# Decoder layer: the next tile's attention scores between a tile's quantised rows and their product with the context

## The chip, the cores and the metric

The kernel runs on one core of a Trainium2 chip. The metric is the device time of one execution in microseconds (us), as the median of several runs. TensorE is PE in the profile, VectorE is DVE, ScalarE is ACT, GpSimd is POOL, and SP is the engine that issues most of the loads.

## The reference, cut to what matters

The input x has 2 x 512 token rows of 1024 numbers. Three stages follow each other, each with a residual and a layer norm:

```python
# 1. attention inside each token, between its 32 "d" positions, over 8 groups of heads
q = einsum('bse,edh->bsdh', x, Wq) + bq          # k, v likewise, repeated 4 times over the heads
attn = softmax(einsum('bsdh,bseh->bsde', q, k) / sqrt(32))
x = layernorm(x + einsum('bsde,bseh->bsdh', attn, v))
# 2. product with the context, both sides rounded to 8 bits
fake_quant = lambda x, s, z: (clip(round(x / s + z), 0, 255) - z) * s
x = layernorm(x + matmul(fake_quant(x), fake_quant(ctx)))     # ctx: 2 x 1024 x 1024
# 3. feed-forward block with a routed part
h = relu(x @ up_w) ** 2                            # 1024 -> 2048
shared = h @ down_w
routed = ((x @ fc1_w) @ expert_w) * (sum of the two largest of x @ gate_w) @ fc2_w
x = layernorm(x + layernorm(shared + routed) * gamma + beta)
```

## The kernel before

**Tiles and blocks.** The 1024 token rows are cut into 8 tiles of 128 rows (one row for each partition). Two tiles make a block, so there are four blocks. Stages 1 and 2 work tile by tile; stage 3 works block by block, for blocks 0 and 1 with plain products (`ffn`), and for blocks 2 and 3 together with fewer, combined products (`ffn_pair`).

**The token path of one tile.** `scores` (L435, L441) multiplies and sums q and k on VectorE in four chunks. `exponentials` (L450, L451, L454) takes the row maximum, subtracts it on VectorE, and takes Exp on ScalarE. `attend` (L458 to L487) sums the exponentials, multiplies them with v on VectorE in four chunks (L466, L472), and adds the result to the tile xc; `normalise_aside` then normalises xc on ScalarE, with a small power on GpSimd. `cross` quantises the rows on ScalarE into `a` (L598), lets a DMA from ScalarE's queue transpose them into `aT` (L601), and multiplies `aT` with the quantised context `cq` on TensorE (L611, the tile py, in two halves). VectorE adds the row sums' share (r at L604, L605) and the product (L615) to xc, and ScalarE normalises again. `hand_over` transposes xc into x2T, the input of the feed-forward products. Tile 1, the last one before block 0 can start, takes another way through `cross`, called hurried: it quantises on VectorE and transposes on TensorE.

**The feed-forward of a block.** `ffn` runs 16 up products (L768, relu and square on ScalarE at L786 and L787), 4 products with fc1 (VectorE multiplies them by the routing at L797), and 20 steps of down products (L982). `finish` then reads the sums on VectorE (L295 to L939).

**What sets the order.** The program is emitted by generators. `token_path` emits tile by tile; `fill` emits the projections of tiles 2 to 7, beside tiles 0 and 1; `ffn` emits a block's products, beside tiles 2 to 7. Each `yield` hands over a weight, meant as microseconds, and a loop advances the token path while its sum of weights times `PACE` is below the sum of the feed-forward's weights. A scheduler then fixes the order on each engine at build time: it prefers what was emitted earlier, but lets later work pass where it believes that the earlier work is not ready. An edge overrides it: instructions traced under `tc.issue_after(x)` stay behind x on x's engine. `behind_products` uses such an edge to keep py behind the last feed-forward product that had been emitted by then.

**Buffers.** py takes a bank from `spare_bank`: of ps_dn while a block's up products run (`phase` "up"), of ps_mm, which has two banks, while its down products run. The up products and the routing take ps_mm banks as well. xc has 6 buffers, prod, s, qk and v two each, and aT and cq one each. The second half of the rows needs a second quantised context: `context_beside` makes it on ScalarE while block 0 runs, once py of tile 3 has been emitted, and tile 4's `cross` is emitted only when it is complete (`made`).

**Loads.** xc(t) is loaded from SP's queue, q, k and v of tile t from GpSimd's queue (`fetch_qkv`), the weights from SP's queue.

Of the kernel before, what the change touches and what calls it, by code (L numbers as in the profile page):

```python
# [9 lines left out]
F32 = mybir.dt.float32  # L10
BF16 = mybir.dt.bfloat16
AF = mybir.ActivationFunctionType
ALU = mybir.AluOpType
# [3 lines left out]
P = 128  # L17
# [10 lines left out]
def kernel(  # L28
# [24 lines left out]
    nc = tc.nc  # L53

    B, S, E = x.shape
    _, D, H = wq.shape
# [11 lines left out]
    NT = B * S // P  # L68
    TB = 2
# [1 line left out]
    NBLK = NT // TB  # L71
    HALF = 512
    DC = 8
    PACE = 0.64
    GW = 32
    NK = NI + NL

# [3 lines left out]
    xf = x.flatten_outer_dims()  # L81
# [4 lines left out]
    xpool = ctx.enter_context(tc.tile_pool(name="xc", bufs=6))  # L86
# [34 lines left out]
    bv_ge = frontp.tile([P, G, D], F32, name="bv_ge")  # L121
# [45 lines left out]
    def new_qkv(t, away):  # L167
        pool, bufs = (attp, KEPT) if away else (tokp, 2)
        qk = pool.tile([P, 2 * DG], F32, tag="s12" if away else "qk", name=f"qk_{t}", bufs=bufs)
        v = pool.tile([P, G, D], F32, tag="s4" if away else "v", name=f"v_{t}", bufs=bufs)  # L170
        return qk, v

    def fetch_qkv(t):
        qk, v = new_qkv(t, False)
        nc.gpsimd.dma_start(qk, qkv_d[t, :, 0 : 2 * DG])
        nc.gpsimd.dma_start(v.rearrange("p g e -> p (g e)"), qkv_d[t, :, 2 * DG :])
        qkv[t] = qk, v
# [48 lines left out]
    qkv = {}  # L226
    xTs = [load_xT(0)]
    ps0 = [projection_psum(t) for t in range(TB)]
    for k in range(KE):
        stage = work.tile([P, E], F32, tag="work", name=f"wq_{k}")  # L230
        nc.sync.dma_start(wqkv[k][:, DG : 2 * DG], wk2[ts(k, P), :])
        last = nc.sync.dma_start(stage, wq2[ts(k, P), :])
# [33 lines left out]
    ns12 = const.tile([P, 1], F32, name="ns12")  # L266
# [3 lines left out]
    s12d2 = const.tile([P, 1], F32, name="s12d2")  # L270
# [157 lines left out]
    def scores(t, qk, behind=None):  # L428
        q3 = qk[:, 0:DG].rearrange("p (d g) -> p d g", g=G)
        k3 = qk[:, DG : 2 * DG].rearrange("p (e g) -> p e g", g=G)  # L430
        s = tokp.tile([P, D, D], F32, tag="s", name=f"s_{t}", bufs=2)
        for c in range(D // DC):
            prod = tokp.tile([P, DC * D * G], F32, tag="prod", name=f"pqk_{t}_{c}", bufs=2)
            with tc.issue_after(behind.ins) if behind is not None else ExitStack():
                nc.vector.tensor_tensor(  # L435
                    prod.rearrange("p (d e g) -> p d e g", d=DC, g=G),
                    q3[:, ts(c, DC), :].unsqueeze(2).to_broadcast([P, DC, D, G]),
                    k3.unsqueeze(1).to_broadcast([P, DC, D, G]),
                    ALU.mult,
                )  # L440
            nc.vector.tensor_reduce(  # L441
                s[:, ts(c, DC), :].rearrange("p d e -> p (d e)"),
                prod.rearrange("p (c g) -> p c g", g=G), AX.X, ALU.add,
            )
            yield 4.6
        return s

    def exponentials(t, s):
        smax = small.tile([P, D], F32, tag="smax", name=f"smax_{t}")
        nc.vector.tensor_reduce(smax, s, AX.X, ALU.max)  # L450
        nc.vector.tensor_tensor(  # L451
            s, s, smax.unsqueeze(2).to_broadcast([P, D, D]), ALU.subtract
        )
        nc.scalar.activation(s, s, AF.Exp, scale=INV_SQRT_D)  # L454

    def attend(t, xc, s, v):
        den = small.tile([P, D], F32, tag="den", name=f"den_{t}")
# [112 lines left out]

        return tc.issue_after(lately[0].ins) if lately[0] is not None else ExitStack()

    def cross(t, xc, cq, crow):
        hurried = t == TB - 1
        tmp = work.tile([P, E], F32, tag="work", name=f"qt_{t}")
        a = attp.tile([P, E], BF16, tag="a", name=f"a_{t}")
        aT = tokp.tile([P, KC, P], BF16, tag="aT", name=f"aT_{t}")
        if hurried:

            quantise(a, xc, tmp, rs1, z1)  # L580
            yield 2.2
            pt = ps_tr.tile([P, KC, P], BF16, tag="tr", name=f"pta_{t}")
            with behind_products():
                for k in range(KC):
                    nc.tensor.transpose(pt[:, k, :], a[:, ts(k, P)], identb)
            nc.scalar.copy(aT, pt)
            yield 1.0
            total = ps_tr.tile([P, 2], F32, tag="tr", name=f"pr_{t}")
            for k in range(KC):
                nc.tensor.matmul(  # L590
                    total, aT[:, k, :], onesb[:, 0:2], start=(k == 0), stop=(k == KC - 1)
                )
            total = total[:, 0:1]
        else:
            total = small.tile([P, 1], F32, tag="total", name=f"total_{t}")
            for _ in below_top(tmp, xc, tmp, rs1, z1):
                pass
            nc.scalar.activation(  # L598
                a, tmp, AF.Identity, scale=-1.0, bias=code_down, accum_out=total
            )  # L600
            nc.scalar.dma_start_transpose(aT, a)  # L601
            yield 12.0
        r = small.tile([P, 1], F32, tag="r", name=f"r_{t}")
        nc.vector.tensor_mul(r, total, s12d2)  # L604
        nc.vector.scalar_tensor_tensor(xc, xc, r, crow, ALU.add, ALU.add)  # L605
        sums = small.tile([P, 2], F32, tag="sum2", name=f"sum2_{t}")
        for h in range(E // HALF):
            py = spare_bank(f"py_{t}_{h}")
            with behind_products():
                for k in range(KC):  # L610
                    crossed[t] = nc.tensor.matmul(  # L611
                        py, aT[:, k, :], cq[:, k, ts(h, HALF)], start=(k == 0), stop=(k == KC - 1)
                    )
            xh = xc[:, ts(h, HALF)]
            nc.vector.scalar_tensor_tensor(  # L615
                xh, py, ns12, xh, ALU.mult, ALU.add,
                accum_out=None if hurried else sums[:, h : h + 1],
            )
        if hurried:
            last = normalise(xc, f"2_{t}")  # L620
            yield 6.0
        else:
            yield 3.0
            last = yield from normalise_aside(xc, sums, f"2_{t}")
            yield 6.0
        return last

    def token_path():


        batch = ahead = None
        for blk in range(NBLK):
            xcs = []
            x2T = []
            for i in range(TB):
                t = blk * TB + i
                xc = xpool.tile([P, E], F32, tag="xc", name=f"xc_{t}")
                nc.sync.dma_start(xc, xf[ts(t, P), :])
                qk, v = qkv.pop(t)
                if 0 < t < NT - 1:  # L640
                    fetch_qkv(t + 1)
                if t == TB:
                    first = last
                if ahead is None:

                    ahead = scores(t, qk, first if t >= TB else None)
                while True:
                    try:
                        step = next(ahead)
                    except StopIteration as done:  # L650
                        s = done.value
                        break
                    yield step
                exponentials(t, s)
                if t < TB:
                    nc.vector.tensor_add(v, v, bv_ge)
                yield 3.1
                ahead = None
                if t == 0:

                    ahead = scores(1, qkv[1][0])
                    yield next(ahead)
                yield from attend(t, xc, s, v)
                if t % (S // P) == 0:
                    b = t // (S // P)
                    while len(made) < (b + 1) * KC:
                        yield 1.0
                    batch = cqs[b], context_row(b, cqs[b])
                last = yield from cross(t, xc, *batch)

                def hand_over(blk=blk, t=t, i=i, xc=xc, x2T=x2T):
                    if not x2T:
                        pool, tag = (attp, "x2T") if blk <= PAIR else (pools["late"], "x2T_late")
                        x2T.append(pool.tile([P, KE, NB], F32, tag=tag, name=f"x2T_{blk}"))
                    with behind_products():
                        transpose_f32(x2T[0][:, :, ts(i, P)], xc, f"x2_{t}")

                    nc.gpsimd.dma_start(xc, ln_beta.partition_broadcast(P), accum_op=ALU.add)

                if t == 0 or up_to[0] < blk or blk > PAIR:
                    held.append((blk, hand_over))
                else:
                    hand_over()
                xcs.append(xc)
            yield blk, xcs, x2T
# [406 lines left out]

    pools = {}
    tokens = token_path()
    rest = fill()

# [28 lines left out]
    for blk in range(PAIR):  # L1127
        while len(ready) <= blk:
            w_tok += advance()
        for weight in ffn(*ready[blk]):  # L1130
            w_ffn += weight
            while alive and w_tok * PACE < w_ffn:
                step = advance()
# [45 lines left out]
```

## Time and profile before

| what | us |
|---|---|
| three runs | 736.18, 737.22, 740.0; median 737.22 |
| the profiled execution | 733.81, of which the span is 731.8 |
| TensorE busy | 696.0 |
| VectorE busy | 545.1 |
| ScalarE busy | 240.0 |
| start of block 0's first up product | 149.7 |
| start of block 1's first up product | 315.5 |
| start of the pair's first product | 474.9 |

The profile is of one execution. Its span runs from the first to the last instruction; the 2 us beside it are the execution's start and end. A row such as "L611 PE MATMUL py<-cq,aT x16" gives the line of the kernel, the engine, the operation, the tile written and the tiles read, and a bracket after it the idle time of that engine just before it, with what ended it. fp32 products show as two records each, so that one up product of 8 matmuls is 16 records.

### The profile page before, as it was taken

The page shows a single profiled execution, that of the slowest core. Times are in us where ns is not written, and L with a number is a line of the kernel's source. Part 1 is how long each engine was busy: PE and PEld are TensorE (multiplying, and loading weights), DVE is VectorE, ACT ScalarE, POOL GpSimd, SP SyncE. Part 2 cuts the span into 40 slices and gives each one's busy share as a digit, 9 for nine tenths or more (in the row PEclk, how much of TensorE's full clock was granted, in tenths as well). Part 3 has the DMA queues.
Part 4 walks back from the last instruction along what each step waited for, and adds up shares of the span by engine and source line. Part 5 has one row for each costly group of instructions (what it writes and reads, how often), then busy time and mean ns, then how long its engine had stood idle before and what let it go on. Part 6 is the DMA issues. An engine that isn't in the chain of part 4 may idle for free. (4 is left out here: it accounts for less than half of the span.)

```text
span 731.8 us, 7278 instructions
## 1 busy us (share of the span) xinstructions
PE 696.0 (95%) x2803; PEld 493.8 (67%) x2812; DVE 545.1 (74%) x619; ACT 240.0 (33%) x389; POOL 64.0 (9%) x96
## 2 busy tenths in 40 slices
PE   6999999999799899999899999999999999999992
PEld 3666654478686344478686444588888888888882
DVE  4799986899989779999899950455454663779736
ACT  2097733222553394428525240311522100000001
POOL 2001211200101020002001000100000000001001
PEclk9999999999999999999999999999999999999996
DMA  8999533785535485456357345441333134555501
GB/s 284 346 297 379 125 45 106 246 285 161 162 116 156 140 256 211 143 167 228 92 168 186 120 169 177 132 109 58 123 107 116 57 116 173 173 173 202 201 1 57
DMA packets 71554, 120.05 MB, mean 164 GB/s; under 512 B 10640, under 2 KB 44944, under 8 KB 71520
## 3 DMA queue, kind: packets, MB, share of 16 engines
q1 hardware_dynamic: 57344, 98.84, 40.0%
q0 software_dynamic: 6496, 18.39, 9.7%
q10 hardware_dynamic: 7680, 2.36, 1.5%
q8 instruction: 22, 0.36, 0.2%
q14 instruction: 12, 0.10, 0.0%
HBM read 106.73 MB, written 11.01 MB: 161 GB/s over the span
## 5 line engine op out<-in xcount | busy, mean ns | idle before, releaser
L982 PE MATMUL pd<-dn,h 128*128 128x512 f32 x320 | 138.8, 592 | 0.0
L768 PE MATMUL pu<-x2T,up 128*128 128x256 f32 x512 | 112.7, 380 | 1.1 <-DMA up<-in_L_ffn_up_w_dram 1.1
L982 PEld LDWEIGHTS pd<-dn,h 128*128 128x128 f32 x320 | 60.5, 190 | 72.9 <-issue 72.2
L768 PEld LDWEIGHTS pu<-x2T,up 128*128 128x128 f32 x512 | 96.6, 190 | 15.7 <-ACT relu L786 1.8
L435 DVE TENSOR_TENSOR pqk<-qk 128x2048 f32<-128x2048 f32 x32 | 72.3, 2283 | 0.0
L441 DVE TENSOR_REDUCE s<-pqk 128x256 f32<-128x2048 f32 x32 | 72.3, 2277 | 0.0
L466 DVE TENSOR_TENSOR pav<-s,v 128x2048 f32<-128x2048 f32 x32 | 72.3, 2280 | 0.0
L472 DVE TENSOR_REDUCE o<-pav 128x64 f32<-128x2048 f32 x32 | 71.9, 2265 | 0.0
L152 PE MATMUL pqk<-wqkv,xT 128*128 128x512 f32 x128 | 65.2, 610 | 1.1 <-DVE wqkv L233 0.8
L1022 DVE TENSOR_TENSOR tt<-dn 128x1024 f32<-128x1024 f32 x20 | 24.3, 1220 | 24.5 <-DMA dn<-in_L_ffn_down_w_dram 15.7
L157 PEld LDWEIGHTS pv<-wqkv,xT 128*128 128x128 f32 x128 | 24.3, 190 | 24.2 <-issue 22.0
L1068 PE MATMUL ps<-dn,h 128*128 128x256 f32 x160 | 40.4, 379 | 0.0
L1068 PE MATMUL ps<-tt,h 128*128 128x256 f32 x160 | 40.4, 379 | 0.0
L1068 PE MATMUL ps<-dn,s 128*128 128x256 f32 x160 | 40.4, 379 | 0.0
L611 PE MATMUL py<-cq,aT 128*128 128x512 bf16 x121 | 29.9, 395 | 10.2 <-DMA aT<-a 9.8
L1080 ACT COPY y<-ps 128x256 f32<-128x256 f32 x4 | 1.5, 373 | 109.9 <-PE ps L1068 109.9
L157 PE MATMUL pv<-wqkv,xT 128*128 128x256 f32 x128 | 35.6, 379 | 0.0
L615 DVE SCALAR_TENSOR_TENSOR xc<-py,ns,xc 128x512 f32<-128x512 f32 x16 | 11.9, 748 | 28.7 <-PE py L611 28.4
L1068 PEld LDWEIGHTS ps<-dn,h 128*128 128x128 f32 x160 | 30.4, 190 | 4.1
L1068 PEld LDWEIGHTS ps<-dn,s 128*128 128x128 f32 x160 | 30.4, 190 | 4.1
L1068 PEld LDWEIGHTS ps<-tt,h 128*128 128x128 f32 x160 | 30.4, 190 | 4.1
L326 POOL TENSOR_TENSOR rstd<-ve,neg_half 128x1 f32<-128x1 f32 x18 | 14.3, 795 | 213.4 <-ACT ve L324 212.6
(204 smaller groups left out, 1022.1 us busy)
## 6 DMA issues: line engine op xcount, KB each, us to landing
dn<-in_L_ffn_down_w_dram SPq DMA_DIRECT2D x32, 1024.0 KB, 5.1
up<-in_L_ffn_up_w_dram SPq DMA_DIRECT2D x16, 1024.0 KB, 5.3
dn<-e SPq DMA_DIRECT2D x8, 1024.0 KB, 5.0
pair<-in_L_ffn_up_w_dram SPq DMA_DIRECT2D x8, 1024.0 KB, 5.3
fc<-in_L_ffn_fc_w_dram SPq DMA_DIRECT2D x6, 1024.0 KB, 5.9
xs<-in_x_dram SPq DMA_DIRECT2D x8, 512.0 KB, 7.2
wq<-in_L_attn_Wq_dram SPq DMA_DIRECT2D x8, 512.0 KB, 5.8
xc<-in_x_dram SPq DMA_DIRECT2D x8, 512.0 KB, 9.6
```

The source lines that it names most:

```text
L152: projecting[0] = nc.tensor.matmul(pqk, xT[:, k, :], wqkv[k][:, 0 : 2 * DG], start=(k == 0), stop=(k == KE - 1))
L157: nc.tensor.matmul(pv[:, :DG], xT[:, k, :], wqkv[k][:, 2 * DG : 3 * DG], start=(k == 0), stop=(k == KE - 1),)
L326: nc.gpsimd.tensor_tensor(rstd, ve, neg_half, ALU.pow)
L435: nc.vector.tensor_tensor(prod.rearrange("p (d e g) -> p d e g", d=DC, g=G), q3[:, ts(c, DC), :].unsqueeze(2).to_broadcast([P, DC, D, G]), ...
L441: nc.vector.tensor_reduce(s[:, ts(c, DC), :].rearrange("p d e -> p (d e)"), prod.rearrange("p (c g) -> p c g", g=G), AX.X, ALU.add,)
L466: nc.vector.tensor_tensor(prod.rearrange("p (d g e) -> p d g e", d=DC, g=G), s[:, ts(c, DC), :].unsqueeze(2).to_broadcast([P, DC, G, D]), ...
L472: nc.vector.tensor_reduce(o[:, ts(c, DC), :].rearrange("p d g -> p (d g)"), prod.rearrange("p (c e) -> p c e", e=D), AX.X, ALU.add,)
L611: crossed[t] = nc.tensor.matmul(py, aT[:, k, :], cq[:, k, ts(h, HALF)], start=(k == 0), stop=(k == KC - 1))
L768: lately[0] = nc.tensor.matmul(ps[:, :NB], ws[:, k, wcols], xT[:, k, :], start=(k == 0), stop=(k == KE - 1))
L982: lately[0] = nc.tensor.matmul(pd[i][n], h[kk // 4][:, i, kk % 4, :], w[:, k, ts(n, HALF)], start=(kk == 0), stop=(kk == NK - 1),)
L1022: nc.vector.tensor_tensor(tt[:, 0:2], w[:, 1], w[:, :, 0], ALU.subtract)
L1068: began[m] = lately[0] = nc.tensor.matmul(banks[m], units[jj][m][:, k, :], weights[gg][m][:, k, :], start=begins and not second, stop=(jj ...
```

## The change

The order of the token path is changed. Before, a tile went through scores, exponentials, attend and cross, and then the next tile began. Now a tile's `cross` quantises its rows and starts their transpose, then emits the whole of the next tile's scores and exponentials (`scores_left`), and only then the row sums, the product py and the additions. The next tile's loads (`begin`: xc(t+1) on SP and q, k, v of tile t+2 on GpSimd) move with the scores. Tile 1 (hurried) keeps its order, so tile 2's scores come after it as before; tile 7 has no next tile and yields 14.0 instead.

On VectorE, edges hold r, L605 and the two L615 of a tile behind the subtraction (L451) of the next tile's exponentials, except for tiles 1 and 7. `PACE` goes from 0.64 to 0.7, and the yield of 12.0 in `cross` becomes 2.0 plus those of the next tile's scores (18.4 and 3.1). No operation is added or removed.

```diff
-    PACE = 0.64
+    PACE = 0.7
...
-        nc.vector.tensor_tensor(
+        lowered[0] = nc.vector.tensor_tensor(
             s, s, smax.unsqueeze(2).to_broadcast([P, D, D]), ALU.subtract
         )
         nc.scalar.activation(s, s, AF.Exp, scale=INV_SQRT_D)
+
+    lowered = [None]
...
-    def cross(t, xc, cq, crow):
+    def cross(t, xc, cq, crow, between):
...
             nc.scalar.dma_start_transpose(aT, a)
-            yield 12.0
+            yield 2.0
+            yield from between
+        behind = ExitStack if hurried or t == NT - 1 else lambda: tc.issue_after(lowered[0].ins)
         r = small.tile([P, 1], F32, tag="r", name=f"r_{t}")
-        nc.vector.tensor_mul(r, total, s12d2)
-        nc.vector.scalar_tensor_tensor(xc, xc, r, crow, ALU.add, ALU.add)
+        with behind():
+            nc.vector.tensor_mul(r, total, s12d2)
+            nc.vector.scalar_tensor_tensor(xc, xc, r, crow, ALU.add, ALU.add)
...
-            nc.vector.scalar_tensor_tensor(
-                xh, py, ns12, xh, ALU.mult, ALU.add,
-                accum_out=None if hurried else sums[:, h : h + 1],
-            )
+            with behind():
+                nc.vector.scalar_tensor_tensor(
+                    xh, py, ns12, xh, ALU.mult, ALU.add,
+                    accum_out=None if hurried else sums[:, h : h + 1],
+                )
...
-        batch = ahead = None
+        batch, last = None, None
+        at, done = {}, {}
+
+        def begin(t):
+            xc = xpool.tile([P, E], F32, tag="xc", name=f"xc_{t}")
+            nc.sync.dma_start(xc, xf[ts(t, P), :])
+            qk, v = qkv.pop(t)
+            if 0 < t < NT - 1:
+                fetch_qkv(t + 1)
+            at[t] = xc, v, scores(t, qk, last if t == TB else None)
+
+        def scores_left(t):
+
+            if t not in at:
+                begin(t)
+            s = yield from at[t][2]
+            exponentials(t, s)
+            if t < TB:
+                v = at[t][1]
+                nc.vector.tensor_add(v, v, bv_ge)
+            done[t] = s
+            yield 3.1
+
...
+                if t not in done:
+                    yield from scores_left(t)
+                xc, v, _ = at[t]
                 if t == 0:
 
-                    ahead = scores(1, qkv[1][0])
-                    yield next(ahead)
-                yield from attend(t, xc, s, v)
+                    begin(1)
+                    yield next(at[1][2])
+                yield from attend(t, xc, done[t], v)
...
-                last = yield from cross(t, xc, *batch)
+                between = scores_left(t + 1) if t + 1 < NT else iter((14.0,))
+                last = yield from cross(t, xc, *batch, between)
```

More of the change, by code (lines that the diff above doesn't have):

```diff
@@ L636, in token_path @@
                 t = blk * TB + i
[L637 to L658, printed above, removed]
+                if t not in done:
+                    yield from scores_left(t)
+                xc, v, _ = at[t]
                 if t == 0:
-                    ahead = scores(1, qkv[1][0])
-                    yield next(ahead)
-                yield from attend(t, xc, s, v)
+                    begin(1)
+                    yield next(at[1][2])
+                yield from attend(t, xc, done[t], v)
                 if t % (S // P) == 0:
```

## The prediction

> **What bounds the kernel now.** I began with the page's first part, busy time by engine.
>
> ```profile
> PE 696.0 (95%) x2803; PEld 493.8 (67%) x2812; DVE 545.1 (74%) x619; ACT 240.0 (33%) x389; POOL 64.0 (9%) x96
> ```
>
> TensorE is busy 696.0 of 731.8 us. A change that takes no matmul away can win only from the 35.8 us in which TensorE is idle, or from its clock. Stretch by stretch the idle time is 6.5 us in the first 25 us (loads), 3.0 between 100 and 130, 1.1 at 157 (a weight), 11.0 between 190 and 400, and 13.7 after 520, in the pair. The tokens run beside TensorE in the 11.0, so the next views are the waits of TensorE (first line) and VectorE, and TensorE's timeline.
>
> ```profile
> PE py L611 <- DMA aT<-a: 9.8, 3, 4.0
> ...
> DVE xc L615 <- PE py L611: 28.4, 8, 18.6
> ...
> DVE den L458 <- ACT s L454: 10.7, 6, 5.4
> ```
>
> ```profile
> 200.83 3.40 PE L611 MATMUL py<-cq,aT 128*128 128x512 bf16 x15 [4.00 <-DMA aT<-a]
> ...
> 249.46 5.31 PE L611 MATMUL py<-cq,aT 128*128 128x512 bf16 x15 [2.79 <-DMA aT<-a]
> ...
> 304.07 3.62 PE L611 MATMUL py<-cq,aT 128*128 128x512 bf16 x16
> ...
> 357.18 3.63 PE L611 MATMUL py<-cq,aT 128*128 128x512 bf16 x15 [2.99 <-DMA aT<-a]
> ...
> 408.64 3.62 PE L611 MATMUL py<-cq,aT 128*128 128x512 bf16 x15
> ```
>
> The bracket is TensorE's idle time and what ended it: the products py of tiles 2, 3 and 5 stand at the head of the queue 4.00, 2.79 and 2.99 us before the transposed rows aT have landed. That is 9.8 of the 11.0 us. Tile 3's product also takes 5.31 us where the others take 3.62; the windows view, whose third column from the end is the granted clock, has 0.60 and 0.50 there:
>
> ```profile
> 249.50:251.00 1.50, 1.37 (x4) 0.62 (x6) 0.00 (x0) 0.00 (x0) 0.00 (x0) 0.60 0.02 6
> 251.00:253.00 2.00, 2.00 (x7) 0.64 (x5) 0.22 (x1) 0.00 (x0) 0.00 (x0) 0.50 0.00 0
> ```
>
> VectorE's waits are longer but cost nothing by themselves: it has finished everything of tile 7 but the product's addition by 440, and TensorE's down product runs to 470 without a gap.
>
> **What the Trainium skill says.** "Perfetto Trace Analysis", Optimization Strategy: find the gaps of the contended engine and make what ends them start sooner. I follow it; the gaps are those above. "TensorE: Matmul & The Clock Gate", Part 1: after an idle window of about 3.4 us the array may fall to half clock, in windows that run freely. The trace agrees in part: half clock beside the 2.79 us wait, none after the 4.00 us one. The same page, Terms and Step-by-step: matmuls keep their order, ScalarE and VectorE are strict first-in-first-out. The trace agrees: a late aT holds all products behind it, and VectorE sat 3.83 us before L615 at 252.78.
>
> **Part 1: where py stands on TensorE.** It is held behind the last FFN product emitted before it (`behind_products`), and the yields say which that is. A yield of 3.5 in `ffn` is 3.5 us of TensorE: 64 records of L768 take 13.98 us, 16 to a product, and 40 of L982 take 17.33, 8 to a step. Before, a tile's yields sum to 72.9, and py(2) comes after 18.4 + 3.1 + 27.4 + 12 = 60.9, times 0.64 = 39.0 FFN units. After, it is 21.5 + 27.4 + 2 + 21.5 = 72.4, times 0.7 = 50.7, and the period is 62.9 x 0.7 = 44.0 for 72.9 x 0.64 = 46.7. Counted with the 1.5 at a block's start, the six py stand before behind up product 11, down step 5, down step 18, up 11, down 4, down 17; the trace has 13, 5, 18, 11, 4, 17, so for tile 2 alone the scheduler went two products past its floor. After: up 15, down 7, down 20, up 12, down 5, down 16. (Tile 4 waits a few units for the second context, which may begin only once py(3) is emitted; with that its py falls just inside block 0's end.) So py moves back by 2, 2, 2, 1 and 1 steps, forward by 1 for tile 7, which had 13 us to spare.
>
> **Part 2: is aT there?** Tile 2: TensorE came at 196.8, aT at 200.8; two products more are 7.0 us, margin 3 us: 4.0 gone. Tile 3: 246.7 - 4.0 + 7.0 = 249.7 against 249.5: 2.8 gone, and I take the 1.7 us of half clock (5.31 - 3.62) as gone with it. Tile 4: 304.1 - 8.5 + 7.0 = 302.6, and aT was there before 304.1. Tile 5 is the tight one: 354.2 - 8.5 + 3.5 = 349.2, where aT came at 357.2. It must come 8 us sooner, and VectorE must bring that.
>
> **Part 3: VectorE and ScalarE.** Moved ahead of a tile's last additions are 4 x (2.28 + 2.28) us of scores, 1.22 of maximum and 1.22 of subtraction: 20.6 us, no operation more or fewer. Behind them wait r (0.16), L605 (1.28) and the two L615 (0.75 each). In the trace the scheduler has most of the scores there already (three quarters of tile 3's scores lie ahead of r at 196.75); what stood behind L615 was the maximum and the subtraction. For tile 4 the subtraction therefore waited 3.83 us for py(3), its Exp then ran at 261.05 behind two passes of context rows, and den waited 5.41 us, to 262.1. Freed of py, the subtraction can end near 250 and den start at 251 to 254, 8 to 11 us sooner. VectorE then runs tile 4, tile 5's scores and tile 5 without another wait of size, so aT(5) lands 0 to 10 us sooner: a wait of 0 to 8 us comes back, I take 1.5. Late next would be L615 itself, hence the normalised tile, but a block's transposes are needed 40 us later.
>
> **Part 4: new holds.** py(4) stands behind the block's last down step and fills both banks of ps_mm. The next block's routing and first up product need them, and they come free by L615, now pinned behind the subtraction of tile 5. That ended at 304.2 and should end near 296; py(4) ends at 306: 0 to 3 us, taken 0.5. On ScalarE the Exp (1.05 us) waits for the subtraction with relu of the up products behind it, which frees TensorE's two banks: a wait up to one product (3.5 us) is covered by the other bank, and before, Exp had waits of 1.6 to 6.8 us without any of TensorE for relu: 0. On VectorE the end of block 0 (7.6 us from 314.5 to 322.1) is queued there too. The moved step also issues DMAs: tile t+1's xc on SP (0.42 us) and tile t+2's qk and v on POOL (0.59 and 0.57 us). On POOL they wait for buffers that are long free then; rstd queues behind them. On SP, xc(6) and xc(7) waited 7.1 and 3.7 us for block 0's end with up weights behind; two weights are loaded ahead (14 us), so nothing, unless block 0's end slips by over 4 us. In the front xc(1) (512 KB) may go earlier while the DMA engines are full: -1 to +1 us, taken 0, since TensorE ran without a load wait from 37 to 106. There the trace already has r(0) (93.06) behind tile 1's subtraction (88.87), so tile 0 changes nothing.
>
> **Sum.** -4.0 - 2.8 - 1.7 - 3.0 + 1.5 + 0.5 = -9.5 us. Profiled: 733.81 - 9.5 = 724.3, span 722.3. The median of the three runs, 737.22, lies 3.4 us above that execution; I apply the difference to it: 727.7 us.
>
> **Rivals.** *Forecast, 0.56:* as summed, 724 to 731. *The wait moves on, 0.26:* VectorE wins nothing, aT(5) comes as late as before and TensorE stands there 6 to 8 us, or it does at tile 3. For it: TensorE's gain itself brings each due time forward. Against: the 5.41 and 3.83 us waits are in front of tile 5. Then -9.5 + 6 = -3.5: 733.7. *The change does little, 0.06:* the scheduler, which already interleaves, puts py where it stood; then 737. Against it: the floor is an edge in the program, not a preference. *Slower, 0.12:* the seam between the blocks. If VectorE passes tile 5's subtraction late, TensorE waits for L615 with the next block's products behind it, VectorE has block 0's end behind the same additions, and SP has up weights behind xc(6). Each us that this subtraction ends after 306 is lost one for one; from 316 all the gain is gone, from 320 it is a loss of 0.5%. It ended at 304.2, so VectorE would have to be 16 us later than before: with another 4 us for a cold clock, 743. Against: no VectorE work is added.
>
> **Numbers.** About 0.5% (3.7 us) is what a measurement here can tell from no change. Half of the second rival falls inside it: faster 0.70, same 0.17, slower 0.13. The likeliest case's own range is 724 to 731. The range 721 to 739 takes in, below, aT waits that all vanish with the small gaps of 0.3 and 0.9 us and some of the 3.0 in the front, and above, the second and third rivals with the spread of the runs shown (736.2 to 740.0).
>
> **What would show it.** Right: the waits have py on aT for under 3 us instead of 9.8; py(2) after 240 records of L768 counted from block 0's start, py(3) after 56 of L982, py(4) after the last of block 0; the wait of den for Exp falls from 10.7 to under 6; the end of the pair is unchanged in shape. Wrong: aT waits of over 5 us at tile 5; a wait of TensorE for L615 at block 1's first products, or for up weights there; VectorE idle before L615 with attention ready behind it and py late for it; a join at tile 7 in which TensorE stands still.

## The result, and the profile after

| what | before | after |
|---|---|---|
| median of four runs each | 736.70 us (735.1 to 740.0) | 725.82 us (724.57 to 726.52) |
| the profiled execution | 733.81 | 725.26 |
| its span | 731.8 | 723.2 |
| first product of block 0 | 149.66 | 152.02 |
| first product of block 1 | 315.49 | 309.90 |
| first product of the pair | 474.87 | 466.21 |

The change makes the kernel faster: the ratio is 0.985, 95% interval 0.981 to 0.988. A second series of the same kernel gave 725.11 against 735.85, ratio 0.985 (0.983 to 0.987). The forecast was 727.7, and 724.3 for the profiled execution.

The last three rows say where the time went. The front (up to block 0) became 2.4 us longer, block 0 8.0 us shorter (165.8 to 157.9), block 1 3.1 us shorter (159.4 to 156.3), and the pair stayed as it was (256.93 to 256.99). The sum is the span's -8.6.

Busy time by engine, kernel after (page, first part): TensorE does the same 696.0 us of work in a shorter span.

```profile
PE 696.0 (96%) x2802; PEld 494.5 (68%) x2812; DVE 545.3 (75%) x619; ACT 239.1 (33%) x389; POOL 63.8 (9%) x96
```

TensorE's waits, kernel after (line, tile, who released it; sum in us, times, longest). The row of py on aT, 9.8 us before, is gone. What stands there now is small, except for the first row, which is new in size and lies in the front:

```profile
PE pe L419 <- DVE xc L623: 2.5, 1, 2.5
...
PE pl L780 <- DVE h L809: 1.0, 1, 1.0
...
PE pu L780 <- ACT lg L737: 0.5, 1, 0.5
...
PE pg L731 <- DVE xc L623: 0.3, 1, 0.3
```

VectorE's waits, kernel after. Its waits for py fall from 28.4 us in 8 to 20.5 in 4 (19.0 of it is tile 7's, off the path), and den's waits for Exp from 10.7 to 4.7:

```profile
DVE xc L623 <- PE py L618: 20.5, 4, 19.0
...
DVE den L460 <- ACT s L454: 4.7, 5, 1.1
```

TensorE's timeline, kernel after (start, duration, instruction; in a bracket the idle time before it). No py of tiles 2 to 6 has a bracket any more, and tile 3's takes 3.62 us where it took 5.31:

```profile
205.88 3.40 PE L618 MATMUL py<-cq,aT 128*128 128x512 bf16 x15
...
251.29 3.62 PE L618 MATMUL py<-cq,aT 128*128 128x512 bf16 x15
...
304.43 3.62 PE L618 MATMUL py<-cq,aT 128*128 128x512 bf16 x15
308.34 1.07 PE L731 MATMUL pg<-x2T,gate 128*32 128x256 f32 x16 [0.29 <-DVE xc L623]
...
352.11 3.40 PE L618 MATMUL py<-cq,aT 128*128 128x512 bf16 x15
...
403.40 3.62 PE L618 MATMUL py<-cq,aT 128*128 128x512 bf16 x15
```

The windows view of the kernel after has 1.00 as the granted clock (third column from the end) in the two stretches that had 0.60 and 0.50, and TensorE busy for 207.46 of the 210 us between 190 and 400:

```profile
249.50:251.00 1.50, 1.50 (x5) 0.67 (x4) 1.50 (x2) 0.00 (x0) 0.00 (x0) 1.00 0.85 295
251.00:253.00 2.00, 1.95 (x9) 0.78 (x8) 2.00 (x3) 0.00 (x0) 0.00 (x0) 1.00 0.66 270
190.00:400.00 210.00, 207.46 (x797) 138.18 (x801) 206.13 (x163) 110.46 (x179) 20.21 (x29) 1.00 0.58 179
```

The same stretch in the kernel before had 198.76 busy:

```profile
190.00:400.00 210.00, 198.76 (x767) 132.61 (x770) 192.00 (x152) 110.30 (x178) 18.86 (x29) 0.99 0.54 168
```

VectorE's timeline, kernel after. L451 is the subtraction of tiles 4, 5 and 6 in turn, L623 the first addition of tile 4 (L615 before), r belongs to tile 5:

```profile
246.45 1.22 DVE L451 TENSOR_TENSOR s<-s,smax 128x1024 f32<-128x1024 f32 x1
...
248.99 1.21 DVE L460 TENSOR_REDUCE den<-s 128x32 f32<-128x1024 f32 x1
...
289.80 1.23 DVE L451 TENSOR_TENSOR s<-s,smax 128x1024 f32<-128x1024 f32 x1
...
307.53 0.74 DVE L623 SCALAR_TENSOR_TENSOR xc<-py,ns,xc 128x512 f32<-128x512 f32 x1
...
342.35 1.23 DVE L451 TENSOR_TENSOR s<-s,smax 128x1024 f32<-128x1024 f32 x1
...
344.96 0.16 DVE L611 TENSOR_TENSOR r<-total,s12d 128x1 f32<-128x1 f32 x1 [1.38 <-ACT a L602]
```

The kernel before had, for tile 4's den and tile 5's r:

```profile
262.12 1.22 DVE L458 TENSOR_REDUCE den<-s 128x32 f32<-128x1024 f32 x1 [5.41 <-ACT s L454]
...
352.99 0.15 DVE L604 TENSOR_TENSOR r<-total,s12d 128x1 f32<-128x1 f32 x1
```

Tile 4's den starts 13.1 us sooner. Tile 5's quantised rows are complete when r starts, 344.96 instead of 352.99: 8.0 us sooner, which is what tile 5 needed.

**Where the front lost 2.4 us.** Here is TensorE's timeline of the kernel before, from tile 0's product to block 0:

```profile
106.23 3.62 PE L611 MATMUL py<-cq,aT 128*128 128x512 bf16 x15
...
112.73 1.13 PE L419 MATMUL pe<-fc,exT 128*128 128x512 f32 x2 [1.12 <-DVE xc L615]
...
116.40 11.43 PE L419 MATMUL pe<-fc,exT 128*128 128x512 f32 x26 [0.38 <-ACT exT L405]
...
149.66 3.72 PE L768 MATMUL pu<-x2T,up 128*128 128x256 f32 x16
```

And of the kernel after:

```profile
112.22 3.40 PE L618 MATMUL py<-cq,aT 128*128 128x512 bf16 x15
118.14 12.05 PE L419 MATMUL pe<-fc,exT 128*128 128x512 f32 x24 [2.52 <-DVE xc L623]
...
152.02 1.35 PE L780 MATMUL pu<-x2T,up 128*128 128x256 f32 x5
```

pe is the product of expert_w with fc1, which the tokens do not need. Tile 0's py now comes 6.0 us later, in the middle of it. It takes both banks of ps_mm, VectorE is busy with tile 1 and reads them only at 117.34, and pe waits 2.52 us for a bank:

```profile
117.34 0.73 DVE L623 SCALAR_TENSOR_TENSOR xc<-py,ns,xc 128x512 f32<-128x512 f32 x1
```

After that wait pe takes 12.05 us for 24 records, 1.5 us more than the same 24 take at full clock (10.57, without the edges and with ones for aT, two experiments below). The half clock is the larger part of the loss: the kernel before waits 1.12 us for the same addition too, and without the edges, where the wait is 2.51 us and the clock stays full, the front from the last projection to block 0 takes 44.25 us, against 43.4 before and 45.7 in the kernel after.

### The profile page after: what moved, and what is told of

It reads as the page before. It is cut to its first block, busy times and chain, and to the rows that moved or that the text cites. A ratio compares the mean times of both kernels' runs of the same rounds, so it can differ in the third digit from the quotient of the medians.

```text
span 723.2 us, 7274 instructions
## 1 busy us (share of the span) xinstructions
PE 696.0 (96%) x2802; PEld 494.5 (68%) x2812; DVE 545.3 (75%) x619; ACT 239.1 (33%) x389; POOL 63.8 (9%) x96
## 5 line engine op out<-in xcount | busy, mean ns | idle before, releaser
L152 PEld LDWEIGHTS pqk<-wqkv,xT 128*128 128x128 f32 x128 | 24.3, 196 | 12.6 <-issue 5.5
L419 PE MATMUL pe<-fc,exT 128*128 128x512 f32 x64 | 29.9, 619 | 2.5 <-DVE xc L623 2.5
```

What stands on the lines that cost most here:

```text
L152: projecting[0] = nc.tensor.matmul(pqk, xT[:, k, :], wqkv[k][:, 0 : 2 * DG], start=(k == 0), stop=(k == KE - 1))
L419: expert[0] = nc.tensor.matmul(ps, exT[:, m, ts(l, P)], fc2[m // 2][:, m % 2, ts(n, HALF)], start=(m == 0), stop=(m == NL - 1),)
```

## The experiments

The theory: the gain is the waits for aT with the cold spell (the time at half clock) behind tile 3's. It needs both halves of the change, py later on TensorE (place) and VectorE ahead (order); the edges keep VectorE's order, and the later py(4) brings a risk at the seam between the blocks. The rivals: the gain lies in something else that moved (transfers, VectorE's waits); one half alone is enough; the edges cost something at the seam. Every ratio is against the kernel before, in the same rounds.

### What the waits are worth

```diff
-                        py, aT[:, k, :], cq[:, k, ts(h, HALF)], start=(k == 0), stop=(k == KC - 1)
+                        py, onesb if t >= TB else aT[:, k, :], cq[:, k, ts(h, HALF)], start=(k == 0), stop=(k == KC - 1)
```

In py of tiles 2 to 7 a constant tile of ones stands in place of aT. The product leaves the tokens' rows out and waits for no transpose; the rest of the program stays. The edit was made in the kernel before:

> The kernel before, in which py of tiles 2 to 7 multiplies the context with the constant tile of ones instead of aT (its output is left wrong for these tiles); transposes, VectorE's and ScalarE's work and their order stay. Theory (the gain is the 9.8 us of waits for aT and the 1.7 us of half clock beside one of them): 11 to 12 us faster than before, no wait of TensorE over 1 us between 190 and 400, all of tile 3's py at full clock. Rival (the waits only stand in for something else that is late, so that TensorE waits elsewhere): less than 6 us faster. Rival for the clock: py(3) stays slow without a wait in front, 9 to 10 us faster.

It took 725.94 us against 736.00, ratio 0.987 (0.985 to 0.989): 10.1 us less, a little under what was expected, and about as fast as the change. Tile 3's product took 3.62 us, so the rival for the clock fell. TensorE's waits in this run show why it isn't 11 to 12. Other things come late when the path runs faster: an up product for its weight, two fc1 products (pl) for h, and a transpose (pt_x) for x2T. The kernel before has 1.1 for the first row, 0.9 for the last, and none for h:

```profile
PE pu L768 <- DMA up<-in_L_ffn_up_w_dram: 2.1, 1, 2.1
PE pl L768 <- DVE h L797: 2.0, 2, 1.5
...
PE pt_x L133 <- ACT x2T L134: 1.3, 1, 1.3
```

The same edit in the kernel after asks whether the change does anything else:

> The changed kernel with the same substitution of ones for aT in py of tiles 2 to 7 (output left wrong for these). Theory: the change has already taken away every wait for aT, so nothing is left: within 0.5 us of the changed kernel, that is 10.5 to 11.5 us faster than before in the median. Rival (waits for aT hide below what the trace names): 1 to 3 us faster than the changed kernel.

It took 727.24 us (ratio 0.990, 0.987 to 0.992), 8.8 us less than before where I had expected 10.5 to 11.5. The kernel after took 725.82 and 725.11, so no wait for aT is left in it. And once the waits are gone from both kernels, in the same rounds, the change gains nothing (727.24 against 725.94): the waits for aT with their cold spell are its whole prize. In the trace two other waits are longer than in the kernel after, pe for L623 in the front (3.27 us) and pg for L623 at the seam (2.00); that they make up the shortfall is not shown, as the runs go from 724.55 to 731.76.

### Each half alone

**Place alone.** The kernel before, with its yields chosen so that py comes where the change puts it:

```diff
+    PLACE = {2: 31.0, 3: 14.0, 4: 10.5, 5: 8.0, 6: 9.5, 7: 0.6}
...
-            yield 12.0
+            yield PLACE.get(t, 12.0)
...
-            yield 3.0
+            yield 0.0 if t == TB else 3.0
             last = yield from normalise_aside(xc, sums, f"2_{t}")
-            yield 6.0
+            yield 0.0 if t == TB else 6.0
```

> The kernel before, its scores left where they were; only the yields ahead of py are changed tile by tile (31, 14, 10.5, 8, 9.5 and 0.6 for tiles 2 to 7 in place of 12), so that py stands behind up 15, down 7, down 20, up 12, down 5 and down 16, as in the changed kernel. Theory (the place of py takes the waits of tiles 2 and 3, VectorE's lead is needed for tile 5): waits for aT at tiles 2 and 3 below 0.5 us, at tile 5 4 to 8 us, in all 2 to 6 us faster than before. Rival A (the place alone is enough): no wait at tile 5, 10 to 12 us faster. Rival B (the scores' order alone matters): as before.

733.37 us, ratio 0.995 (0.993 to 0.996). The single runs go from 729.1 to 735.2, and the trace is of one of the slower ones (734.32). In it py of tiles 2, 3, 4, 6 and 7 stands where it does in the kernel after; tile 5's came a product later. TensorE's timeline of this run:

```profile
204.96 3.40 PE L613 MATMUL py<-cq,aT 128*128 128x512 bf16 x15
...
303.82 3.62 PE L613 MATMUL py<-cq,aT 128*128 128x512 bf16 x16
...
312.97 1.93 PE L721 MATMUL pg<-x2T,gate 128*32 128x256 f32 x16 [5.54 <-DVE xc L617]
...
365.03 5.09 PE L613 MATMUL py<-cq,aT 128*128 128x512 bf16 x15 [2.23 <-DMA aT<-a]
```

Tiles 2 and 3 no longer wait. Tile 5 still does, 2.23 us (I had expected 4 to 8) and then half clock (5.09 instead of 3.4 to 3.6), although its py starts 50.2 us into block 1 where the change has it at 42.2. The size was as expected, its main place was not: more is lost at the seam, where py(4) holds both banks and the routing pg waits 5.54 us for their addition (L617), then runs cold too (1.93 instead of 1.07).

**Order alone.** The kernel after with the old pace:

```diff
-    PACE = 0.7
+    PACE = 0.64
```

> The changed kernel with PACE 0.64 in place of 0.7. By the count of the yields py then stands behind up 13, down 5, down 18, up 9, down 1 and down 11, so for tiles 2 and 3 where it stood before the change, and for tiles 5 to 7 two to six steps earlier. Theory (place against aT): waits for aT of 2 to 4 us at tiles 2 and 3, of 6 to 10 us at tile 5, and at tile 6 too; 735 to 745, no better than before. Rival (the order of the scores brings the gain, the pace is a detail): 725 to 729.

729.45 us, ratio 0.992 (0.989 to 0.995). I had expected 735 to 745, and this failed. TensorE's timeline of this run:

```profile
202.29 5.31 PE L618 MATMUL py<-cq,aT 128*128 128x512 bf16 x16 [2.95 <-DMA aT<-a]
...
249.88 3.62 PE L618 MATMUL py<-cq,aT 128*128 128x512 bf16 x16
...
348.02 3.62 PE L618 MATMUL py<-cq,aT 128*128 128x512 bf16 x16
```

py stands where it stood before the change for tiles 2 to 4 and two to six steps earlier for tiles 5 to 7, yet only tile 2 waits: its scores stand where they stood, so it gains nothing from the order. From tile 3 on VectorE's lead brings aT soon enough; for tile 5 it was there at 348.0, where the kernel before had it at 357.2. By the medians the order is the larger half (5.4 us against 2.6), although its run also carries the loss in the front (a wait of 2.52 us there); the two intervals overlap, so the clock alone does not show it.

**Pace alone.** The kernel before with `PACE = 0.7`:

> The kernel before with PACE 0.7. py stands behind up 12 to 13, down 7, then just inside block 1 for tile 4, up 16, down 10, and tile 7 has its product emitted only after all of block 1. Theory: the waits of tiles 3 and 5 go, that of tile 2 (4 us) stays, and tile 7's product, its normalisation and transposes stand open behind block 1's last down step, a gap of 8 to 12 us of TensorE at the join: 734 to 742. Rival (the pace alone does it): 725 to 729.

751.76 us, ratio 1.021 (1.018 to 1.024): slower, and beyond the 734 to 742 at which I had put it. TensorE's waits of this run:

```profile
PE py L611 <- DMA aT<-a: 14.2, 3, 9.9
...
PE pt_x L133 <- ACT xc L331: 4.2, 1, 4.2
PE py L611 <- DVE y L932: 3.4, 1, 3.4
```

At the old yields the larger pace pushes the whole path back. py(4) slides over the seam into block 1, where it waits for a bank of ps_dn that block 0's finish still holds (3.4). Tile 7's aT is 9.9 us late when all of block 1's products have been given out, its normalised rows (xc, from which x2T is made) come 4.2 us late after that, and nothing is left to cover either.

So pace alone costs 2.1%, place alone gives 0.5%, order alone 0.8%, both together 1.5%.

### The edges, and the seam

The kernel after, without the edges on VectorE:

```diff
-        behind = ExitStack if hurried or t == NT - 1 else lambda: tc.issue_after(lowered[0].ins)
+        behind = ExitStack
```

> The changed kernel without the edges that hold r, L612 and L623 behind the next tile's subtraction; the scores' place in the program and the pace stay, and so does TensorE's order. Theory (the edges give VectorE its lead; the emission order gives most of it already): aT at tile 5 still in time or up to 2 us late, 0 to 2 us slower than the changed kernel, 9 to 11 us faster than before. Rival (the edges cost time at the seam between the blocks, L623 behind 20 us of scores): 0.5 to 1.5 us faster than the changed kernel.

729.38 us, ratio 0.992 (0.990 to 0.994), 3.6 us slower than the kernel after where I had expected 0 to 2. TensorE's instructions stand in the same order as in the kernel after, and no aT is late. The wait is at the seam, on TensorE's timeline:

```profile
312.30 1.73 PE L731 MATMUL pg<-x2T,gate 128*32 128x256 f32 x16 [3.70 <-DVE xc L623]
```

and VectorE's timeline of the same run shows the cause. Without the edge r stands first and waits for a, the subtraction of tile 5 comes 5.1 us later than the 289.80 of the kernel after, and L623 4.0 us later than 307.53:

```profile
293.54 0.16 DVE L611 TENSOR_TENSOR r<-total,s12d 128x1 f32<-128x1 f32 x1 [2.58 <-ACT a L602]
294.87 1.23 DVE L451 TENSOR_TENSOR s<-s,smax 128x1024 f32<-128x1024 f32 x1
...
311.49 0.74 DVE L623 SCALAR_TENSOR_TENSOR xc<-py,ns,xc 128x512 f32<-128x512 f32 x1
```

The rival, that the edges cost time at the seam, fell: they save about 3.6 us (729.38 against 725.8).

If the seam is the cause, moving py(4) alone two down steps earlier must bring this back:

```diff
-            yield 2.0
+            yield -9.5 if t == 4 else 2.0
             yield from between
...
-            yield 3.0
+            yield 14.5 if t == 4 else 3.0
             last = yield from normalise_aside(xc, sums, f"2_{t}")
```

> The changed kernel without the edges, and with py of tile 4 two down steps earlier, at step 18 of block 0 in place of 20 (11.5 units of weight taken ahead of it and given back behind it). Theory (what the edges save, 3.6 us by the runs before, is the wait of block 1's routing for L623 at the seam and the cold clock behind it, because py of tile 4 stands right at the seam): that wait falls from 3.7 us to under 0.5, the time comes back to 725 to 727. Rival (without the edges VectorE is late everywhere): 729 to 730 as without the edges alone.

727.22 us, ratio 0.990 (0.988 to 0.993): 2.2 us less than without the edges alone, just above the 725 to 727 expected. The two intervals overlap, so the clock supports the seam as the cause without settling it. On TensorE's timeline of this run pg has lost its bracket, and an up product now waits for relu:

```profile
308.23 1.07 PE L731 MATMUL pg<-x2T,gate 128*32 128x256 f32 x16
...
321.48 3.72 PE L780 MATMUL pu<-x2T,up 128*128 128x256 f32 x16 [1.62 <-ACT relu L798]
```

### The front

The kernel after, with tile 0 alone in the old order:

```diff
-            yield 2.0
-            yield from between
+            if t == 0:
+                yield 12.0
+            else:
+                yield 2.0
+                yield from between
```

> The changed kernel, with tile 0 alone back in the old order (a yield of 12 ahead of its product, tile 1's scores after it); tiles 2 to 7 and the edges as changed. Theory (the 2.4 us by which block 0 starts later than before come from tile 0's product standing behind the first expert products and holding both ps_mm banks until L623 at 117.3): block 0's first up product back at 149 to 150, no wait of an expert product for L623 over 1.5 us, 2 to 3 us faster than the changed kernel, about 723. Rival (the late start is the half clock at 118 to 121 or tile 1's own chain, which comes by chance): block 0 starts at 151.5 to 152.5 again, within 1 us of the changed kernel.

724.64 us against 734.81, ratio 0.987 (0.984 to 0.990), profiled 724.15. The front came as expected: from the end of the projections to block 0 it takes 43.5 us, as before (43.4), where the kernel after takes 45.7. The median, 1.2 us below the 725.82 of the kernel after where I had expected 2 to 3, can't show so little across different rounds. It was run again beside the kernel after:

> The changed kernel itself once more, on the chip and in the rounds of the next three. All theories: 0.983 to 0.987 of before, block 0's first up product 45.7 us behind the end of tile 7's projection (in the trace of the changed kernel 106.3 to 152.0).

> Once more the changed kernel with tile 0 in the old order, now in the rounds of the changed kernel. Theory (2.3 us of the front are tile 0's product behind the first expert product): 1.5 to 2.5 us faster than the changed kernel, block 0's first up product 43.4 us behind the end of tile 7's projection. Rival (the front's loss is made good later, since TensorE finds fewer holes there): within 0.5 us of the changed kernel.

The kernel after took 725.11 us (ratio 0.985, 0.983 to 0.987) with its wait of 2.51 us in the front again; with tile 0 in the old order it was 724.19 (ratio 0.984, 0.982 to 0.986), front 43.4 us. The profiled span was 3.0 us less (721.2 against 724.2), the median only 0.9 where I had expected 1.5 to 2.5, and the intervals overlap: by the clock this stays open.

Which part of the new tile 0 costs? The banks can be tested by themselves, with the order left as the change has it:

```diff
-            py = spare_bank(f"py_{t}_{h}")
+            if t == 0:
+                py = ps_dn.tile([P, HALF], F32, tag="dn", name=f"py_{t}_{h}")
+            else:
+                py = spare_bank(f"py_{t}_{h}")
```

> The changed kernel, with the two banks of tile 0's product taken from ps_dn in place of ps_mm, so that the expert products keep theirs; tile 0's order as changed. Theory (the loss in the front is the expert product's wait of 2.5 us for L623, by the banks, and the half clock behind it): that wait goes, block 0 starts 1.5 to 2.5 us sooner, as with tile 0 in the old order. Rival (the loss is tile 1's own chain, whose power on GpSimd at 121.4 stands behind tile 0's): the expert products run earlier, TensorE then waits for tile 1's rows, block 0 starts at most 0.5 us sooner.

722.84 us (722.44 to 723.83), ratio 0.983 (0.981 to 0.984): in these rounds 2.3 us less in the median than the kernel after, whose runs (723.23 to 726.11) reach a little into its range. The profiled span is 720.5, the shortest of all. TensorE's timeline of this run:

```profile
112.68 3.18 PE L621 MATMUL py<-cq,aT 128*128 128x512 bf16 x14
115.70 7.03 PE L419 MATMUL pe<-fc,exT 128*128 128x512 f32 x16
124.07 3.70 PE L419 MATMUL pe<-fc,exT 128*128 128x512 f32 x8 [1.34 <-ACT e L423]
...
149.60 3.72 PE L783 MATMUL pu<-x2T,up 128*128 128x256 f32 x16
```

All but one of py's records stand as late as in the kernel after (112.68), pe runs on right behind them at full clock but for a wait of 1.34 us for e, and block 0 starts at 149.60; the front takes 42.9 us instead of 45.7. VectorE still waits 3.07 us for the power of tile 1's normalisation on GpSimd, as in the kernel after (before 0.66), and that costs nothing: the rival, that this chain sets the front, fell. The Trainium skill, "Perfetto Trace Analysis", Optimizing Tensor Performance, wants independent groups of products to rotate through different banks, so that the reading of one lies beside the next; this run agrees, with a wait of 2.52 us that goes when py leaves the two banks that pe needs. This version's median is the lowest of all. That it is faster than the kernel after rests on the traces' fronts; the clock alone, with ranges that overlap a little, comes short of showing it.

Last, tile 0 in the old order and py(4) two down steps earlier together:

> The changed kernel with tile 0 in the old order and with py of tile 4 two down steps earlier, edges kept. Theory (the small waits at the seam, 0.3 us for L623 and 0.5 us for the routing's copy, come from tile 4's product at the block's end): 0.3 to 1 us faster than with tile 0 in the old order alone, so 2 to 3.5 us faster than the changed kernel. Rival (two steps earlier aT of tile 4 is late): a wait for aT at tile 4, no faster or up to 3 us slower than tile 0 in the old order.

724.55 us, ratio 0.985 (0.983 to 0.986): no faster than tile 0 alone, where I had expected 0.3 to 1 us. The seam's 0.3 and 0.5 us went, and waits of 0.8 and 0.2 for relu and 0.4 for h came in their place. The rival's late aT at tile 4 did not appear.

## Why the prediction was right

**Part 1, the place, held in full.** On the trace py(2) follows 240 records of up products (15), py(3) 56 of down products (7), py(4) the whole of block 0 (160), py(5) 192 (12), py(6) 40 (5) and py(7) 128 (16).

**Part 2, the waits, held for tiles 2 to 4.** The terms for block 0 sum to -8.0 with the seam (-4.0 - 2.8 - 1.7 + 0.5), and block 0 became 8.0 us shorter. The traces account for 7.7 of that: TensorE's idle time in the block falls from 8.3 us to 2.3, and 1.7 of half clock goes.

**Tile 5's term was too cautious.** The 1.5 us of new wait that I took did not come. Block 1 became 3.1 us shorter, not 1.5. The run with the order alone suggests how much room there was: there py(5) started without a wait at 348.0, and in the kernel after it came at 352.1.

**Part 3, VectorE's lead, held.** I had put tile 4's subtraction near 250 and its den at 251 to 254; they came at 246.5 and 249.0, so den gained 13.1 us where I had forecast 8 to 11. The 8 us for aT(5) came (8.0 at r).

**Part 4, the seam: right in size, wrong in its threshold.** I took 0.5 us, and 0.3 for L623 with 0.5 for the routing that follows were measured. But the rule behind it, that each us is lost once tile 5's subtraction ends after 306, was off by some 15 us. L623 does not follow the subtraction directly: most of tile 5's attention and the start of block 0's finish stand between, 16.2 to 17.7 us from the start of one to the start of the other in three runs. In a fourth, with ones for aT, it is 19.4, since tile 5's den waits there 2.76 us for Exp.

| kernel | subtraction of tile 5 | L623 (or its like) of tile 4 | TensorE's wait |
|---|---|---|---|
| after | 289.80 | 307.53 | 0.29 |
| without the edges | 294.87 | 311.49 | 3.70 |
| place alone | 296.02 | 312.17 | 5.54 |
| after, ones for aT | 289.58 | 309.02 | 2.00 |

In the kernel after, the subtraction ends at 291.0 and TensorE waits 0.29 us, so the loss begins at about that time. Ending near 296, as I forecast, it would have cost about the 3.7 us of the run without the edges, where it ends at 296.1. VectorE came 5 us sooner than that, and so the term came out right: two errors cancelled, which is luck. The rival that ends slower had its place right, and its point of decision far too far out.

**Unforeseen.** A product with fc1 waits 1.0 us for h (L809) in block 1: VectorE, hardly idle there, is now sometimes the later one.

**The front was the term that failed.** "Tile 0 changes nothing" was a term put at 0 that measured +2.4 us. I had looked only at r(0), which already stood behind tile 1's subtraction, and not at what py(0) moves past on TensorE, nor at who needs its two banks. In the kernel after it comes in the middle of pe. The experiment with other banks shows the cause to be the banks, through the wait and the half clock behind it. That miss and the 1.5 us at tile 5 partly cancel, so that the span's -8.6 came close to the sum's -9.5 in part by luck.

**From the execution to the median.** The profiled execution was forecast 1.0 us too low (724.3 against 725.26), the median 1.9 too high. I had carried the 3.4 us between the two over to the new kernel, where they lie 0.6 apart.

**The rivals.** "The wait moves on" fell: no py waits for aT. "The change does little" fell with the positions. "Slower at the seam" did not happen, but the runs without the edges and with the place alone show that it was near.

## What to carry to other kernels

A product that waits at the head of an in-order queue can be helped from both ends, by standing later and by having its operand sooner; measure each alone, since here the later place alone gave 0.5% and the order alone 0.8%, and a coarse knob such as the pace lost 2.1%. For each product that is moved, ask which banks it takes, which instruction empties them, and what stands ahead of that instruction on its engine: every wait of over 2 us that the runs added in the front and at the seam between blocks 0 and 1 was such a bank. Where an order on VectorE carries a gain, an edge that fixes it can be worth more than it costs; here it kept 3.6 us.

## What the runs showed of the hardware

I had not expected how little idle time is enough for half clock, and how uneven it is. The Trainium skill, "TensorE: Matmul & The Clock Gate", Part 1, puts the idle window at about 3.4 us, in windows that run freely. Half clock followed waits of 2.23 us (place alone), 2.51 and 2.52 (the kernel after, twice), 2.79 (before), 2.95 (order alone), 3.38 and 3.79 (pace alone), 3.70 (without the edges) and 5.54 us (place alone). It did not follow 2.51 (without the edges, front), 2.99 and 4.00 (before), nor 3.27 us (after, with ones for aT). Two waits in the front make the plainest pair. The first line is of the kernel after, run again, the second of the run without the edges:

```profile
118.44 12.26 PE L419 MATMUL pe<-fc,exT 128*128 128x512 f32 x24 [2.51 <-DVE xc L623]
...
119.91 10.57 PE L419 MATMUL pe<-fc,exT 128*128 128x512 f32 x24 [2.51 <-DVE xc L623]
```

The same 24 products take 1.7 us more after a wait of the same length. Windows that run freely would fit that, though no run here shows the windows themselves; a length of 3.4 us as the least idle time doesn't fit. A spell cost 1.5 us in the front, 1.7 at tile 3 of the kernel before and 2.9 at tile 2 with the pace alone (6.55 instead of 3.62), so a wait of over 2 us is best priced with up to 3 us on top, and a chance that it doesn't come.
